# The last tile's middle row on ScalarE and accumulating transfers, and TensorE's first tile added by VectorE

## The chip, the cores and the metric

The kernel runs on one core of a Trainium2 chip. The metric is the device time of one execution in microseconds, taken as a median over runs. The engines are named as in the profile: PE (TensorE, with PEld for its weight loads), DVE (VectorE), ACT (ScalarE), POOL (GpSimd) and SP (SyncE, which here only issues transfers). [...]

## The reference, cut to what matters

The input is `x` of shape (16, 384, 32, 32) in fp32. Two layers follow each other:

```
x = x + attention(groupnorm32(x))     # qkv, 8 heads of 48, softmax over 1024 positions, projection, bias
x = x + depthwise7x7(groupnorm32(x))  # w_sym = mean of the weight's four rotations, padding 3
```

Group norm takes mean and variance over 12 channels times 1024 positions of one image. Because the symmetric weights are a mean over four rotations, a tap and its mirror image are equal under a half turn, and the kernel uses that to halve the multiplications.

## The kernel before, in words

An image has 1024 positions (N) and its 384 channels are three tiles of 128 partitions, so a tile `(b, k)` is 128 x 1024 in fp32, 512 KB. A hand-written planner issues the work: `catch_up` and `tap` hand out VectorE's queue, `after` puts a function at a due time, `conv_piece` hands out TensorE's part of the convolution, and loops of the kind "while something is not there, catch_up" hold back what is issued next. Each engine then runs its own queue strictly in this order, and waits on semaphores between engines.

Attention of image b overlaps with the convolution of image b-1. What concerns this document is the tail: when the last image's attention is done, its convolution has no more attention to hide behind. The three tiles of the last image, and one of the image before it, are handled in two ways.

- Three tiles, `PE_TILES` = (14, 2), (15, 2) and (15, 1), are convolved on TensorE. `conv_load` has SP issue eight transfers a half tile (`sh`), `conv_on_pe` runs 28 small matmuls for each half a = 0, 1 of a tile into PSUM (`ps_conv`), `conv_take` has ScalarE copy the half to SBUF (`rows`), and `conv_perm` brings its rows into order with four matmuls against a permutation (`ps_rows`). For (14, 2) and (15, 2) ScalarE then writes the result into `conv` and POOL issues a transfer that adds it into the tile `x1`, and SP stores the tile. For the last one, (15, 1), `conv_add` has VectorE add the result into `x1` in four pieces, and ACT issues the two halves of the store.
- The tile `LAST` = (15, 0) is convolved on VectorE by `fold_ops`. `sides` are three sums (later differences) of the padded tile shifted left and right by j = 1, 2, 3. For the middle row (dy = 0) of the kernel the centre product and three products of the sides are added into the output `out_t` (which is `x1s[LAST]`). For the rows dy = 1, 2, 3 the even part gathers in `rows_e` (first product by ScalarE in `fold_first`, three more by VectorE in `into`), and `shifted` adds it into `out_t` shifted up and shifted down. The odd part gathers in `rows_o` and is added one way and subtracted the other way.

The last image's group norm is folded in afterwards. The convolution runs on the raw `x1`, and at the end it is scaled by `sc[:, k, 0]`, while a border term carries the mean. Statistics: `st.moments` on ScalarE (two passes for each of three tiles), `st.average` on TensorE (seven one-column matmuls, twice), `spread_of` on VectorE between the two, then `scale_of` with a power on POOL, then `factors`, which adds the border to `ends["x"]` (the tile `rest`, a copy of the padded tile) by an accumulating transfer. `other_borders` does the same for (15, 2) and (15, 1). `whole` is VectorE's pass `out_t * scale + rest`. In the kernel before it stands in the middle of the last list of operations, and what is added after it (two row pairs) carries the scale or its negative (`minus`) as a factor.

`fast_end` writes the order of all this. Its part before the change that the prediction follows:

```
fold_first(n, 0)
st.moments(padded_view(n), 0)            # then the other two tiles, then the copy "rest"
while pe_conv[0][0] < b: conv_piece(False)     # the rest of (14, 2)
conv_piece(False)                              # (15, 2), first half
st.average(late["masks"], 0, mean)             # first statistics
conv_piece(False)                              # (15, 2), second half, taps 0 to 4
st.average(late["masks"], NK, st.d)            # second statistics
for p in first: conv_perm(*p)                  # rows of (14, 2)
```

Of the kernel before, what the change touches and what calls it, by code (L numbers as in the profile page):

```python
# [10 lines left out]
F32 = mybir.dt.float32  # L11
# [5 lines left out]
P = 128  # L17
# [28 lines left out]
def kernel(  # L46
# [96 lines left out]
    def run(general):  # L143
        tag = "g" if general else "f"
        with ExitStack() as stack:
# [706 lines left out]
            def fold_ops(b, k, i):  # L852
# [16 lines left out]
                scale = []  # L869

                def shifted(src, dy, op, half=None):
                    lo, hi = max(0, -dy) * W, (H - max(0, dy)) * W
                    if half is not None:
                        lo, hi = (lo, N // 2) if half == 0 else (N // 2, hi)
                    dst, src = out_t[:, lo:hi], src[:, lo + dy * W : hi + dy * W]
                    if scale:
                        w = scale[0] if op == ALU.add else scale[1]
                        vec.scalar_tensor_tensor(dst, src, w, dst, ALU.mult, ALU.add)
                    else:
                        vec.tensor_tensor(dst, dst, src, op)  # L880
# [17 lines left out]
                if (b, k) == LAST:  # L898
                    outs.append((ts, lambda: first(grid(out_t), padded_view(i), e(0, 0))))
                else:  # L900
                    outs.append((full, lambda: into(grid(out_t), padded_view(i), e(0, 0))))
# [25 lines left out]
                if (b, k) == LAST:  # L927
                    outs.pop()
                    for half in range(2):
                        outs.append(  # L930
                            (
                                0.7,
                                lambda half=half: (
                                    shifted(rows_o[0], -PAD, ALU.subtract, half),
                                    half_store(b, k, half),
                                ),
                            )
                        )
# [16 lines left out]
                if (b, k) == LAST:  # L955

                    def begin(n, dy, j):
                        nc.scalar.activation(rows_o[n], sides[slot[j]], AF.Identity, scale=o(dy, j))  # L958
# [5 lines left out]
                    def minus_begin():  # L964
# [3 lines left out]
                    ops = [op for op in ops if op[1] not in [f for _, f in (*sums[12:], *outs[10:])]]  # L968
# [3 lines left out]
                        (full, lambda: (sums[14][1](), other_borders()), None),  # L972
# [155 lines left out]
            def conv_perm(b, k, a):  # L1128

                nonlocal clock  # L1130
                if a == 0:
                    return
                pss[b, k] = psum(f"ps_rows_{b}_{k}")
                for half in range(2):
                    part = slice(64 * half, 64 * half + 64)
                    for row in range(2):
                        nc.tensor.matmul(
                            pss[b, k][part, row, :],
                            lhsT=perm[:, row],
                            rhs=shs[b, k][:, half, :],  # L1140
                            start=True,
                            stop=True,
                        )
# [5 lines left out]
                if b == B - 1:  # L1149
                    while "borders" not in late:  # L1150
                        catch_up(now() + 0.5)
                    nc.scalar.activation(
                        by_rows(t), grids(pss[b, k]), AF.Identity, scale=ends["st"].sc[:, k, 0:1]
                    )
                else:
                    nc.scalar.copy(by_rows(t), grids(pss[b, k]))
# [422 lines left out]
            def conv_piece(rows=True):  # L1579
# [14 lines left out]
                elif a and (b, k) == PE_TILES[-1]:  # L1594
                    conv_take(b, k, 0)
# [62 lines left out]
            def fast_end(b):  # L1658
# [11 lines left out]
                fold_first(n, 0)  # L1670
                st.moments(padded_view(n), 0)
# [9 lines left out]
                loads(1)  # L1681
                conv_piece(False)
# [7 lines left out]
                catch_up(clock)  # L1690
                st.average(late["masks"], NK, st.d)
# [164 lines left out]
```

## Time and profile before

| | us |
|---|---|
| median of 3 runs | 2836.43 (2835.36 to 2836.66) |
| the profiled execution's own time | 2835.83 |
| its span, first to last instruction | 2834.1 |
| what lies around the span | 1.7 |
| start of the last image's convolution on VectorE (first `side`) | 2781.46 |
| end of `conv_add`, the last work of an engine | 2826.01 |

In the profile a line of the timeline gives the start in us, the duration, the engine and source line, the operation, output and input, the count, and in brackets the time that the engine stood idle just before and what ended the idling. SPq, ACTq and POOL with DMA_DIRECT2D are issues of transfers. A count of 56 on PE is 28 matmul instructions, since an fp32 one is recorded twice. Successive instructions of one engine overlap by some 0.1 us, so costs are better read from start to start.

| stretch of the tail (us) | PE busy | DVE busy | ACT busy | DMA share |
|---|---|---|---|---|
| 2781.00 to 2804.20 | 23.20 | 23.06 | 14.56 | 0.51 |
| 2804.20 to 2811.00 | 6.80 | 6.73 | 3.67 | 0.51 |
| 2811.00 to 2829.90 | 13.31 | 13.85 | 7.53 | 0.90 |

### The profile page before, as it was taken

The numbers are of one execution on the slowest core, as the hardware profiler recorded it, in microseconds if no ns is written. First come the engines' busy times: TensorE is split into PE (matmuls) and PEld (weight loads), VectorE is DVE, ScalarE is ACT, GpSimd is POOL, SyncE is SP. The second block draws the span as 40 slices with busy tenths as digits, with TensorE's granted clock in tenths as the row PEclk, the third lists the DMA queues.
The fourth block names the chain that finished last, engine by engine and source line by source line (L and its number), as shares of the span: only waits on it lengthen the run. The fifth ranks groups of instructions, "written<-read, shape, count | busy, mean of one in ns | idle before, by whom it ended". The sixth has DMA issues, their size and how long they took to land. (4 is left out here: it accounts for less than half of the span.)

```text
span 2834.1 us, 46121 instructions
## 1 busy us (share of the span) xinstructions
PE 2822.4 (100%) x19344; PEld 1118.1 (39%) x19344; DVE 2080.6 (73%) x2266; ACT 1664.3 (59%) x1954; POOL 277.6 (10%) x450
## 2 busy tenths in 40 slices
PE   9999999999999999999999999999999999999998
PEld 5343343433434334343443434334343343434433
DVE  4503968959598595976959689595985959769788
ACT  3637647375574756647476473755747566474653
POOL 4201011310100001010010100101000010100111
PEclk9999999999999999999999999999999999999999
DMA  6522131211212112131120302112121121211224
GB/s 240 187 38 49 31 78 27 54 50 45 64 32 44 50 44 65 34 71 35 38 64 27 82 24 51 50 45 64 32 44 50 44 65 34 65 42 37 72 72 136
DMA packets 75562, 168.21 MB, mean 59 GB/s; under 512 B 32368, under 2 KB 34352, under 8 KB 73808
## 3 DMA queue, kind: packets, MB, share of 16 engines
q0 software_dynamic: 33856, 111.00, 15.1%
q1 hardware_dynamic: 40912, 53.11, 6.9%
q8 instruction: 154, 2.52, 0.4%
q10 hardware_dynamic: 576, 1.05, 0.1%
q14 instruction: 64, 0.52, 0.1%
HBM read 112.37 MB, written 27.43 MB: 49 GB/s over the span
## 5 line engine op out<-in xcount | busy, mean ns | idle before, releaser
L642 ACT ACTIVATE e<-ps_s 128x1024 f32<-128x1024 f32 x1024 | 1021.3, 1029 | 448.0 <-PE ps_s L634 447.4
L634 PE MATMUL ps_s<-qk 48*64 48x512 f32 x8192 | 1034.5, 589 | 0.0
L654 PE MATMUL acc<-e,v 64*64 64x512 f32 x8192 | 1034.0, 588 | 0.0
L861 DVE TENSOR_TENSOR side<-padded 128x1024 f32<-128x1024 f32 x270 | 329.8, 1222 | 339.7 <-ACT padded L832 339.7
L864 DVE SCALAR_TENSOR_TENSOR rows_e<-side,even,rows_e 128x1024 f32<-128x1024 f32 x405 | 510.5, 1276 | 85.6 <-ACT rows_e L843 84.0
L654 PEld LDWEIGHTS acc<-e,v 64*64 64x64 f32 x8192 | 308.9, 132 | 571.6 <-issue 571.4
L634 PEld LDWEIGHTS ps_s<-qk 48*64 48x64 f32 x8192 | 307.6, 132 | 574.7 <-issue 525.3
L563 PE MATMUL ps_qk<-x,wqk 128*128 128x512 f32 x1152 | 501.2, 593 | 0.0
L563 PEld LDWEIGHTS ps_qk<-x,wqk 128*128 128x128 f32 x1152 | 217.6, 190 | 276.7 <-issue 272.2
L880 DVE TENSOR_TENSOR x<-x,rows_e 128x992 f32<-128x992 f32 (+2 forms) x270 | 312.0, 1156 | 0.0
L880 DVE TENSOR_TENSOR x<-x,rows_o 128x992 f32<-128x992 f32 (+2 forms) x266 | 305.6, 1149 | 3.0
L570 ACT COPY qk<-ps_qk 128x1024 f32<-128x1024 f32 x96 | 97.2, 1012 | 318.6 <-PE ps_qk L563 318.5
L589 PE MATMUL ps_v<-wv,x 128*128 128x384 f32 x768 | 252.6, 486 | 0.0
L715 PE MATMUL ps_proj<-o,wp 128*128 128x512 f32 x540 | 234.2, 592 | 0.0
L609 ACT COPY v<-ps_v 64x384 f32<-64x384 f32 x256 | 121.4, 474 | 122.6 <-PE ps_v L589 120.0
L589 PEld LDWEIGHTS ps_v<-wv,x 128*128 128x128 f32 x768 | 145.9, 190 | 108.2 <-issue 14.3
L990 POOL DMA_DIRECT2D out<-x x44 | 24.8, 564 | 1543.0 <-DVE x L880 1542.5
L864 DVE SCALAR_TENSOR_TENSOR rows_o<-side,odd,rows_o 128x1024 f32<-128x1024 f32 x135 | 172.8, 1280 | 2.0 <-ACT rows_o L958 0.5
L864 DVE SCALAR_TENSOR_TENSOR x<-side,even,x 128x1024 f32<-128x1024 f32 x135 | 172.8, 1280 | 0.0
L715 PEld LDWEIGHTS ps_proj<-o,wp 128*128 128x128 f32 x540 | 102.6, 190 | 126.2 <-issue 118.4
L723 ACT ACTIVATE x<-ps_proj,bp 128x1024 f32<-128x1024 f32 x45 | 50.1, 1113 | 167.6 <-PE ps_proj L715 167.6
L843 ACT ACTIVATE rows_e<-padded,even 128x1024 f32<-128x1024 f32 x135 | 146.8, 1166 | 0.0
(178 smaller groups left out, 1049.2 us busy)
## 6 DMA issues: line engine op xcount, KB each, us to landing
x<-in_x POOLq DMA_DIRECT2D x90, 512.0 KB, 5.4
inv<-inv SPq DMA_DIRECT2D x126, 256.0 KB
out<-x POOLq DMA_DIRECT2D x44, 512.0 KB, 2.9
xs<-in_x POOLq DMA_DIRECT2D x42, 512.0 KB, 6.7
qk<-qk POOLq DMA_DIRECT2D x96, 128.0 KB, 4.1
o<-o SPq DMA_DIRECT2D x180, 32.0 KB
sh<-v SPq DMA_DIRECT2D x32, 128.0 KB
x<-in_x SPq DMA_DIRECT2D x6, 512.0 KB
```

What stands on the lines that cost most here:

```text
L563: nc.tensor.matmul(ps[:, h, :], lhsT=wqk[:, k, s, t, :], rhs=xns[b][:, k, h * HALF : (h + 1) * HALF], start=(k == 0), stop=(k == NK - 1),)
L570: nc.scalar.copy(halves(qks[u][:, s, :]), ps)
L589: nc.tensor.matmul(ps[:, j, 0:C], lhsT=xns[b][:, k, t * P : (t + 1) * P], rhs=wv[:, k, :], start=(k == 0), stop=(k == NK - 1),)
L609: nc.scalar.copy(dst[:, :, 0 : HEADS // 2 * (D + 1)].rearrange("p k (h d) -> p k h d", d=D + 1)[:, :, :, 0:D], src.rearrange("p k (h d) -> ...
L634: nc.tensor.matmul(ps[64 * c : 64 * c + 64, a, :], lhsT=qk[r, 1, 64 * kb : 64 * kb + 64], rhs=qk[r, 0, h * HALF : (h + 1) * HALF], start=True,
L642: nc.scalar.activation(es[n], ps, AF.Exp, scale=SCALE)
L654: nc.tensor.matmul(accs[a][64 * j : 64 * j + 64, :], lhsT=v[rows, kb, c : c + 64], rhs=e[rows, j, :], start=(kb == 0), stop=(kb == 2 * NT ...
L715: nc.tensor.matmul(ps[:, h, :], lhsT=wp[:, t, o * P : (o + 1) * P], rhs=os_[b, t // 2][:, t % 2, h * HALF : (h + 1) * HALF], start=(t == 0 ...
L843: nc.scalar.activation(grid(rows_e[dy - 1]), padded_view(i), AF.Identity, scale=even[:, k, dy, 0:1],)
L861: vec.tensor_tensor(grid(sides[n]), padded_view(i, j), padded_view(i, -j), op)
L864: vec.scalar_tensor_tensor(dst, src, w, dst, ALU.mult, ALU.add)
L880: vec.tensor_tensor(dst, dst, src, op)
```

## The change

All edits lie in the tail, behind the last softmax step; up to there both kernels issue the same instructions.

1. The middle row of `LAST`: the centre product is now one ScalarE activation into `x1s[LAST]`, and the three products of the sides are ScalarE activations into tiles of their own (`row_1`, `row_2`, `row_3`), all ahead of `st.moments`. Three accumulating transfers of POOL sum them: `row_1` into x1, `row_3` into `row_2`, and when both have landed `row_2` into x1. VectorE no longer takes part.
2. The order of VectorE's list for `LAST`: three sums, nine even row sums, then the three differences, then the shifted adds. The factor pass `whole` goes to the end, in two halves with a store each, so all shifted adds before it are plain adds and the negative factor goes.
3. Tile (14, 2): in place of four matmuls, a copy and an accumulating transfer, `conv_rows_by_dma` has SP issue 16 transfers of 32 KB from `rows` into a tile `planes`, and `rows_add` has VectorE add that into x1 behind the two halves of `whole`; SP's store of the tile comes after it.
4. `conv_perm`'s two loops over rows and halves are exchanged.
5. TensorE's pieces of the second half of a last-image tile: taps 0 to 2, 2 to 4, 4 to 7 in place of 0 to 4, 4 to 7. The first of them comes ahead of the first statistics, the second between first and second statistics, and the third after the second statistics, once the scale has been issued.
6. `other_borders` is issued after the adds of the second odd row instead of at its beginning.

The diff, cut to its core:

```diff
-                def shifted(src, dy, op, half=None):
+                def shifted(src, dy, op):
                     lo, hi = max(0, -dy) * W, (H - max(0, dy)) * W
...
-                def whole():
-
-                    scale.extend((ends["st"].sc[:, k, 0:1], ends["minus"]))
-                    vec.scalar_tensor_tensor(out_t, out_t, scale[0], ends["x"], ALU.mult, ALU.add)
+                    dst = out_t[:, lo:hi]
+                    vec.tensor_tensor(dst, dst, src[:, lo + dy * W : hi + dy * W], op)
+
+                def whole(h):
+
+                    half, s = slice(h * HALF, (h + 1) * HALF), ends["st"].sc[:, k, 0:1]
+                    vec.scalar_tensor_tensor(
+                        out_t[:, half], out_t[:, half], s, ends["x"][:, half], ALU.mult, ALU.add
+                    )
...
+                    def row_product(j):
+                        t = flat(epool.tile([P, 2, HALF], F32, tag="e", name=f"row_{j}"))
+                        nc.scalar.activation(t, sides[j - 1], AF.Identity, scale=e(0, j))
+                        ends["row", j] = t
+                        if j == 1:
+                            nc.gpsimd.dma_start(out_t, t, accum_op=ALU.add)
+                        if j == 3:
+                            nc.gpsimd.dma_start(ends["row", 2], t, accum_op=ALU.add)
+                            nc.gpsimd.dma_start(out_t, ends["row", 2], accum_op=ALU.add)
...
-                    ops = [op for op in ops if op[1] not in [f for _, f in (*sums[12:], *outs[10:])]]
+                    ops = [(*f, {0: "x", 3: "rows"}.get(n)) for n, f in enumerate(sums[:12])]
                     ops += [
                         (full, lambda: side_begin(2, 0, 1), None),
                         (full, lambda: side_begin(3, 1, 2), None),
-                        (full, lambda: (sums[14][1](), other_borders()), None),
+                        (*sums[14], None),
+                        *((*outs[n], None) for n in range(4, 8)),
                         (*sums[16], None),
                         (*sums[18], None),
                         (*outs[10], None),
                         (full, minus_begin, None),
-                        (full, whole, None),
-                        (*outs[12], None),
+                        (*outs[8], None),
+                        (*outs[9], None),
+                        (full, lambda: (outs[12][1](), other_borders()), None),
                         (*outs[13], None),
                         (*sums[20], None),
-                        *((*f, None) for f in outs[14:]),
+                        (*outs[14], None),
+                        (full, lambda: shifted(rows_o[0], -PAD, ALU.subtract), None),
+                        *((0.7, lambda h=h: (whole(h), half_store(b, k, h)), None) for h in range(2)),
+                        (full, rows_add, None),
                     ]
...
+            def rows_add():
+
+                b, k = PE_TILES[0]
+                dst = by_rows(x1s[b, k])
+                nc.vector.tensor_tensor(dst, dst, grids(ends["planes"]), ALU.add)
+                store(b, k, slice(0, N), nc.sync)
...
+                if (b, k) == PE_TILES[0]:
+                    conv_rows_by_dma(b, k)
+                    return
                 pss[b, k] = psum(f"ps_rows_{b}_{k}")
-                for half in range(2):
-                    part = slice(64 * half, 64 * half + 64)
-                    for row in range(2):
+                for row in range(2):
+                    for half in range(2):
+                        part = slice(64 * half, 64 * half + 64)
                         nc.tensor.matmul(
...
+            def conv_rows_by_dma(b, k):
+
+                rows = epool.tile([P, 2, HALF], F32, tag="e", name=f"planes_{b}_{k}")
+                for half in range(2):
+                    for i in range(NG // 2):
+                        for row in range(2):
+                            first = 2 * CG * i + CG * (1 - row)
+                            nc.sync.dma_start(
+                                rows[64 * half + i : 64 * half + 64 : NG // 2, row, :],
+                                shs[b, k][first : first + CG, half, :],
+                            )
+                ends["planes"] = rows
...
-                    pe_conv.extend(((b, k, 0, 0, KS), (b, k, 1, 0, 4), (b, k, 1, 4, KS)))
+                    pe_conv.extend(((b, k, 0, 0, KS), (b, k, 1, 0, 2), (b, k, 1, 2, 4), (b, k, 1, 4, KS)))
                 loads(2)
                 fold_first(n, 0)
+                nc.scalar.activation(
+                    grid(x1s[LAST]), padded_view(n), AF.Identity, scale=even[:, 0, 0, 0:1]
+                )
+                while "row" not in ends or active[0][2] < 3:
+                    catch_up(vclock + 0.5)
+                for f in ends["row"]:
+                    f()
                 st.moments(padded_view(n), 0)
...
                 loads(1)
+                first = [perms.popleft() for _ in range(2)]
+                conv_piece(False)
                 conv_piece(False)
                 catch_up(clock)
                 mean, var = st.first
                 st.average(late["masks"], 0, mean)
...
-                after(1.5, 0.6, lambda: st.spread_of(mean, var))
-                first = [perms.popleft() for _ in range(2)]
+                after(4.5, 0.6, lambda: st.spread_of(mean, var))
                 conv_piece(False)
                 catch_up(clock)
+                while not hasattr(st, "d"):
+                    catch_up(now() + 0.5)
                 st.average(late["masks"], NK, st.d)
...
-                minus = st.more[:, 2 * NK :]
-                nc.vector.tensor_scalar(minus, st.sc[:, 0, 0:1], -1.0, None, ALU.mult)
-                ends.update(minus=minus, st=st)
+                ends.update(st=st)
```

More of the change, by code (lines that the diff above doesn't have):

```diff
@@ L867, in first @@
                     vec.tensor_scalar(dst, src, w, None, ALU.mult)
-                scale = []
-                def shifted(src, dy, op, half=None):
+                def shifted(src, dy, op):
                     lo, hi = max(0, -dy) * W, (H - max(0, dy)) * W
[L873 to L880, printed above, removed]
-                def whole():
-                    scale.extend((ends["st"].sc[:, k, 0:1], ends["minus"]))
-                    vec.scalar_tensor_tensor(out_t, out_t, scale[0], ends["x"], ALU.mult, ALU.add)
+                    dst = out_t[:, lo:hi]
[5 more added lines that the diff above has]
+                    )
                 def e(dy, dx):
@@ L897, in fold_ops @@
                     sums.append((full, lambda j=j: side(j, j - 1, ALU.add)))
[L898 to L901, printed above, removed]
+                outs.append((full, lambda: into(grid(out_t), padded_view(i), e(0, 0))))
                 for j in (1, 2, 3):
@@ L926, in fold_ops @@
                     out_rows(lambda n=n: rows_o[n % 2], dy, ALU.subtract)
-                if (b, k) == LAST:
-                    outs.pop()
-                    for half in range(2):
[L930 to L938, printed above, removed]
                 behind = [0, 1, 2, 3, 6, 6, 9, 9, 12, 12, 17, 17, 19, 19, 21, 21, 21]
@@ L955, in fold_ops @@
                 if (b, k) == LAST:
+                    ends["row"] = [lambda j=j: row_product(j) for j in (1, 2, 3)]
+                    def row_product(j):
[7 more added lines that the diff above has]
+                            nc.gpsimd.dma_start(out_t, ends["row", 2], accum_op=ALU.add)
                     def begin(n, dy, j):
@@ L1132, in conv_perm @@
                     return
+                if (b, k) == PE_TILES[0]:
+                    conv_rows_by_dma(b, k)
+                    return
                 pss[b, k] = psum(f"ps_rows_{b}_{k}")
-                for half in range(2):
-                    part = slice(64 * half, 64 * half + 64)
-                    for row in range(2):
+                for row in range(2):
+                    for half in range(2):
+                        part = slice(64 * half, 64 * half + 64)
                         nc.tensor.matmul(
@@ L1147, in conv_perm, with conv_out @@
                     return
-                t = tpool.tile([P, N], F32, tag="t", name=f"conv_{b}_{k}")
[L1149 to L1156, printed above, removed]
+                while "borders" not in late:
+                    catch_up(now() + 0.5)
+                conv_out(b, k, pss[b, k])
+            def conv_rows_by_dma(b, k):
[9 more added lines that the diff above has]
+                ends["planes"] = rows
+            def conv_out(b, k, rows):
+                t = tpool.tile([P, N], F32, tag="t", name=f"conv_{b}_{k}")
+                nc.scalar.activation(
+                    by_rows(t), grids(rows), AF.Identity, scale=ends["st"].sc[:, k, 0:1]
+                )
                 nc.gpsimd.dma_start(x1s[b, k], t, accum_op=ALU.add)
@@ L1593, in conv_piece @@
                     perms.append((b, k, a))
-                elif a and (b, k) == PE_TILES[-1]:
+                elif a and not first and (b, k) == PE_TILES[-1]:
                     conv_take(b, k, 0)
@@ L1667, in fast_end @@
                     conv_begin(st, b, k)
-                    pe_conv.extend(((b, k, 0, 0, KS), (b, k, 1, 0, 4), (b, k, 1, 4, KS)))
+                    pe_conv.extend(((b, k, 0, 0, KS), (b, k, 1, 0, 2), (b, k, 1, 2, 4), (b, k, 1, 4, KS)))
                 loads(2)
                 fold_first(n, 0)
+                nc.scalar.activation(
+                    grid(x1s[LAST]), padded_view(n), AF.Identity, scale=even[:, 0, 0, 0:1]
+                )
+                while "row" not in ends or active[0][2] < 3:
+                    catch_up(vclock + 0.5)
+                for f in ends["row"]:
+                    f()
                 st.moments(padded_view(n), 0)
@@ L1686, in fast_end @@
                 clock += 1.6
-                after(1.5, 0.6, lambda: st.spread_of(mean, var))
-                first = [perms.popleft() for _ in range(2)]
+                after(4.5, 0.6, lambda: st.spread_of(mean, var))
                 conv_piece(False)
                 catch_up(clock)
+                while not hasattr(st, "d"):
+                    catch_up(now() + 0.5)
                 st.average(late["masks"], NK, st.d)
```

## The prediction

> **What bounds the kernel now.** The page first: the edits all lie behind the last softmax step, so its whole-run shares only say that TensorE is never idle for long.
>
> ```profile
> span 2834.1 us, 46121 instructions
> PE 2822.4 (100%) x19344; PEld 1118.1 (39%) x19344; DVE 2080.6 (73%) x2266; ACT 1664.3 (59%) x1954; POOL 277.6 (10%) x450
> ```
>
> The chain of waits is one piece long (DVE L1167), so I read the timeline of the tail engine by engine. TensorE (start, duration, work):
>
> ```profile
> 2780.71 16.41 PE L1111 MATMUL ps_conv<-sh,mat 128*32 128x464 f32 x158
> 2797.05 1.72 PE L389 MATMUL ps_st_x<-mo_x,wv 128*128 128x1 f32 x14
> 2798.71 3.48 PE L1111 MATMUL ps_conv<-sh,mat 128*32 128x512 f32 x32
> 2802.12 1.72 PE L389 MATMUL ps_st_x<-d_x,wv 128*128 128x1 f32 x14
> 2803.77 1.94 PE L1137 MATMUL ps_rows<-rows,perm 128*64 128x512 f32 x8
> 2805.65 2.63 PE L1111 MATMUL ps_conv<-sh,mat 128*32 128x496 f32 x24
> 2815.77 5.90 PE L1111 MATMUL ps_conv<-sh,wqk 128*32 128x512 f32 x56
> 2821.60 2.70 PE L1137 MATMUL ps_rows<-rows,perm 128*64 128x512 f32 x8
> ```
>
> From 2780.7 to 2824.3 each piece starts where the last ends: no hole. VectorE at the end, and the last issues of POOL and ScalarE's queue:
>
> ```profile
> 2822.53 1.31 DVE L878 SCALAR_TENSOR_TENSOR x<-rows_o,mo_x,x 128x416 f32<-128x416 f32 x2
> 2824.35 1.66 DVE L1167 SCALAR_TENSOR_TENSOR x<-ps_rows,sc_x,x 128x256 f32<-128x256 f32 x4 [0.50 <-PE ps_rows L1137]
> 2820.33 0.85 POOL L1157 DMA_DIRECT2D x<-conv  x1 [3.87 <-DVE x L878]
> 2823.22 4.15 ACTq L1171 DMA_DIRECT2D out<-x  x4
> ```
>
> The final add (conv_add) waits 0.50 us for TensorE. So TensorE's dense run sets the end, with VectorE only 0.5 behind; from the add's end (2826.0) stores and closing take 8.1 us to the span's end. Work taken from VectorE alone buys at most 0.5. ScalarE is the engine that I read as spare, and it is where the change puts work:
>
> ```profile
> 2782.63 3.25 ACT L843 ACTIVATE rows_e<-padded,even 128x1024 f32<-128x1024 f32 x3
> 2785.78 1.06 ACT L318 ACTIVATE sq_x<-padded 128x1024 f32<-128x1024 f32 x1
> 2793.73 1.05 ACT L1675 COPY rest<-padded 128x1024 f32<-128x1024 f32 x1
> 2794.69 1.06 ACT L1126 COPY rows<-ps_conv 128x512 f32<-128x512 f32 x2
> 2797.21 0.58 ACT L1126 COPY rows<-ps_conv 128x512 f32<-128x512 f32 x1 [1.47 <-PE ps_conv L1111]
> 2810.27 2.18 ACT L958 ACTIVATE rows_o<-side,odd 128x1024 f32<-128x1024 f32 x2
> ```
>
> Before 2797.2 it is packed; its only slack there is the 1.47 us ahead of the copy of tile (15,2)'s first half.
>
> **VectorE.** Costs start to start. Removed: the L867 product (0.67), three L864 into x (3 x 1.20), the minus factor (0.1); two 960-wide L878 become plain adds (1.22 to 1.07 each: 0.3), the 928-wide ones also (2.5 to 2.1: 0.4). Added: rows_add, priced as L861's add of the same size, 1.13. The factor pass of 1.28 becomes two halves: 0. Sum: -4.0 us.
>
> **TensorE.** One block of four rows matmuls goes (2803.77 to 2805.65): -1.9. The loop in conv_perm is turned: for the last tile, three of four matmuls (it was two) now follow the copy of the second half; 1.94/4 gives +0.5. The convolution piece of (15,2), second half, is cut in two (0 to 2, 2 to 4), and the first cut moves ahead of the first statistics. In the changed kernel's instruction order that first cut waits for ScalarE's copy of the same tile's first half (one PSUM tile holds both halves). Before, that wait was covered by the statistics block; now nothing stands in front of it.
>
> **When ScalarE gets there.** Ahead of the moments it now has the first product (as L843: 3.15/3 = 1.05) and three row products (as L958: 2.18/2 = 1.09 each): +4.3. What followed moves with it: the moments start at 2790.1 instead of 2785.78, `rest` at 2798.05, (14,2)'s two copies at 2799.0, and (15,2)'s first half at about 2800.0 to 2800.55. TensorE finishes that half at 2797.05 and stands until 2800.6: **+3.5 us**. From there 8 matmuls (1.7), statistics (1.7), 8 more (1.7), second statistics at 2805.7 (2802.12 before), and the rest packed as before without the one block: last rows matmuls at 2823.3 (2821.60 before). Sum for TensorE: +3.5 - 1.9 + 0.5 = +2.1; conv_add starts at 2826.5, ends at 2828.1.
>
> VectorE's 4.0 us are lost on the way: it has its nine row sums and three differences done at 2799.3, then waits for the accumulating transfers and for the statistics that TensorE delivers at 2804.2, and again for L406 at 2807.5. It reaches conv_add at about 2823.3, three microseconds early, with rows_add inside that slack.
>
> **The transfers.** POOL issues three accumulating transfers in place of one (0.87 each). The third needs both others landed, so POOL stands for 5 us with nothing behind it until the factor's power at 2807.6: 0. The row is the landing of such a 512 KB transfer here: 5.4 us (L1157), 5.6 to 7.6 (L1722, two at once). The third product is written at 2790.2; at 5.4 twice the middle row is complete at 2801.0, at 7.6 twice at 2805.4. The trace of before has none beside the 32 `sh` loads (DMA share 0.51 from 2781 to 2804), so I take 5.4 to 6.6: 2801 to 2803.4. [...] It matters only past 2804.0: VectorE's add behind it (1.1) and the spread (0.5) must be done when TensorE asks at 2805.7. So 0 in the sum, and +1.4 at the far end.
>
> SP issues 16 small transfers behind the loads, from 2804.2. The rows lie between 0.34 (L1171) and 0.59 us (L1090) an issue: done by 2810 to 2814, wanted at 2822: 0; past 2822 each microsecond late eats the 3 us of slack first. If transfers in flight hold them up, +2 is the bound.
>
> Stores: ScalarE's border for (15,2) now stands behind its second copy and a product that needs VectorE's 2813.3; it ends at 2815.9 (POOL issued it at 2814.17), so the two accumulations and (15,2)'s store behind it move by +1.8, within the +2.1. (14,2)'s store, at 2811.7 before, goes behind that one: 0.5 MB more after 2827. Moved at the 347 GB/s of the last stretch it is 1.4 us; half-hidden beside the closing I take +0.4, bounds -1 (one of the four ACTq issues was long, 1322 ns, and may be short next time) and +1.4.
>
> **Sum.** +2.1 + 0.4 = +2.5 on the profiled execution's 2835.83: 2838.3. The median shown (2836.43) is 0.6 above that execution: **2838.9**.
>
> [...] Granted clock by stretch (stretch and its length, busy time of PE, PEld, DVE, ACT and POOL, granted clock, DMA share, GB/s):
>
> ```profile
> 8.46:11.88 3.42, 3.02 (x26) 2.62 (x24) 1.29 (x7) 0.00 (x0) 1.57 (x6) 1.00 1.04 397
> 11.88:15.29 3.41, 3.41 (x9) 2.74 (x9) 2.26 (x8) 1.24 (x1) 2.65 (x4) 0.50 0.41 97
> 2797.05:2803.77 6.72, 6.72 (x64) 4.21 (x60) 6.65 (x9) 0.58 (x1) 0.00 (x0) 1.00 0.52 173
> 2827.87:2834.10 6.23, 0.00 (x0) 0.00 (x0) 0.00 (x0) 0.00 (x0) 0.00 (x0) 0.50 0.22 78
> ```
>
> Today the tail keeps 1.00 and falls to 0.50 only 3.5 us after the last matmul. [...] But row two shows a halved window after one with 3.02 us of mostly one-column matmuls, so low work can suffice, and the hole with 1.7 us of statistics behind it is such a stretch. One halved window costs up to 1.7 us: 2840.6. I leave it out of the number and in the range.
>
> **Rivals.**
> - *Clock halves in the hole*, as just priced: about 2840.6. For: rows two and four. Against: the second statistics block of today did not trip it.
> - *Middle row lands late (slower).* Place: the first shifted add into x, ahead of the spread in VectorE's queue. It decides from a landing at 2804.0. Beside loads that already hold half of the DMA time, the three transfers could take 7.6 each with the second queued behind the first by 2 us: 2807.5, so TensorE waits 3.5 more, and in a second hole the clock is likelier to fall. +2.5 + 3.5 = 2842.4, with the clock 2844.1. Against: the loads use only 0.51 of the time and their data are wanted late.
> - *The copy does not hold TensorE* (ScalarE shorter than I price it): -1.9 + 0.5 + 0.4 = -1.0, 2835.4. The full -4.0 of VectorE, if nothing else were late, would be 2832.4, still within 0.2%, so a gain past 0.2% has no working here.
>
> **Numbers.** 0.2% is 5.7 us, about what a measurement of this kernel can tell from no change: faster is below 2830.8, slower above 2842.1. Forecast 0.43; clock 0.21 (a quarter of it with the DMA bounds past 2842.1); late landing 0.25 (nearly all slower); no hold 0.11 (up to 0.04 faster, for what I can't see). Together faster 0.04, same 0.66, slower 0.30. Range 2834.5 to 2845.0: below lies most of the no-hold case's far end, above the landings past 2807 with the clock down.
>
> **What would show it.** In the changed profile: a hole of about 3.5 us on TensorE before the first cut of (15,2), ended by ScalarE's rows copy; second statistics near 2805.7; conv_add waiting some 3 us, not 0.5, for TensorE; the middle row's landing between 2801 and 2803.4; clock 1.00 throughout. Wrong if TensorE has no hole there, if VectorE and not TensorE ends last, or if the first shifted add starts after 2804.

## The result, and the profile after

The changed kernel takes 2842.87 us (median of 8 runs, 2841.74 to 2846.84), the kernel before on the same chip 2835.89 (8 runs, 2835.06 to 2836.76). The measured ratio, which is not simply that of the two medians (1.0025), is 1.0028, with a 95% interval of 1.0019 to 1.0038. So it is slower by 7.0 us, clear of no change, and the lower end of the interval lies just under the 0.2% that the prediction took as the bound of its classes. The profiled execution took 2841.74 (before 2835.83), with a span of 2840.0 (before 2834.1), so the profile has 5.9 of the 7.0 us to explain.

TensorE in the timeline of the changed kernel's tail (start, duration, work, and in brackets the idle time ahead):

```profile
2780.72 16.41 PE L1115 MATMUL ps_conv<-sh,mat 128*32 128x464 f32 x158
2800.46 3.29 PE L1115 MATMUL ps_conv<-sh,mat 128*32 128x512 f32 x16 [3.33 <-DMA sh<-v]
2803.68 1.93 PE L389 MATMUL ps_st_x<-mo_x,wv 128*128 128x1 f32 x14
2805.54 1.84 PE L1115 MATMUL ps_conv<-sh,mat 128*32 128x480 f32 x16
2807.53 1.72 PE L389 MATMUL ps_st_x<-d_x,wv 128*128 128x1 f32 x14
2809.18 2.62 PE L1115 MATMUL ps_conv<-sh,mat 128*32 128x496 f32 x24
2825.13 2.71 PE L1144 MATMUL ps_rows<-rows,perm 128*64 128x512 f32 x8
```

There is a hole where the dense run was unbroken before, and behind it 16 matmul records that take 3.29 us where the next 16 take 1.84. Stretch by stretch (PE, PEld, DVE, ACT and POOL busy, granted clock, DMA share, GB/s), with the edges put where the granted clock changes:

```profile
2797.30:2800.71 3.41, 0.25 (x4) 0.16 (x8) 2.81 (x3) 3.41 (x8) 0.85 (x1) 1.00 0.68 208
2800.71:2804.13 3.42, 3.42 (x19) 0.89 (x11) 0.00 (x0) 1.78 (x2) 0.00 (x0) 0.50 1.03 195
2804.13:2807.54 3.41, 3.26 (x30) 1.82 (x30) 1.65 (x5) 0.00 (x0) 0.00 (x0) 1.00 0.76 206
```

The clock is halved for one stretch of 3.41 us. In the same stretch VectorE does nothing at all (0.00 us busy), and the DMA engines are busy throughout (share 1.03). The other queues, from the timelines of ScalarE, VectorE, POOL and SP:

```profile
2798.86 1.55 ACT L1130 COPY rows<-ps_conv 128x512 f32<-128x512 f32 x3
2805.82 1.19 DVE L872 TENSOR_TENSOR x<-x,rows_e 128x992 f32<-128x992 f32 x1 [5.71 <-DMA x<-row]
2827.92 1.23 DVE L986 TENSOR_TENSOR x<-x,planes 128x1024 f32<-128x1024 f32 x1 [2.51 <-DMA planes<-rows]
2829.06 1.65 DVE L1187 SCALAR_TENSOR_TENSOR x<-ps_rows,sc_x,x 128x256 f32<-128x256 f32 x4
2799.32 0.85 POOL L947 DMA_DIRECT2D x<-row  x1 [8.11 <-DMA row<-row]
2818.68 0.86 POOL L1750 DMA_DIRECT2D x<-border  x1 [3.58 <-ACT border L1749]
2824.30 0.85 POOL L1177 DMA_DIRECT2D x<-conv  x1 [3.37 <-DVE x L872]
2781.08 29.39 SPq L1094 DMA_DIRECT2D sh<-v  x32
2810.57 12.27 SPq L1166 DMA_DIRECT2D planes<-rows  x16
2830.91 1.93 SPq L1191 DMA_DIRECT2D out<-x  x2
```

The same queues before, SP's loads and POOL's issue of the border of (15, 2):

```profile
2781.07 23.07 SPq L1090 DMA_DIRECT2D sh<-v  x32
2814.17 0.85 POOL L1722 DMA_DIRECT2D x<-border  x1 [2.64 <-ACT border L1721]
```

Three chains come in late, one behind the other by a microsecond or so:

- **TensorE.** Hole, halved clock: its last rows matmuls end at 2827.84, 3.5 us later than before (2824.30).
- **Planes.** SP's loads last until 2810.5 (before 2804.1), the 16 plane transfers stand behind them, the last lands at 2827.84 by the trace's semaphore events. `rows_add` waits 2.51 us for it and holds `conv_add` 1.2 us longer than TensorE does. `conv_add` ends at 2830.71 (before 2826.01: +4.7).
- **Border and stores.** POOL issues the border of (15, 2) at 2818.68 (before 2814.17). The second accumulation into the same tile, L1177, waits for that border to land. The profile names VectorE there, but the instruction's waits are for the border's landing and for ScalarE's product; the border's landing, at 2823.79, is the later. L1177 lands at 2830.86, SP's store of (15, 2) goes at 2830.91 and (14, 2)'s behind it; the last store lands at 2836.3 (before 2830.9: +5.4).

`conv_add` is 4.7 us later, the time from there to the last landing 0.7 longer, and the closing after that landing 0.5 longer: 5.9. Why the closing grew stays open.

### The profile page after: what moved, and what is told of

Read it like the earlier page. It is cut to its first block, busy times and chain, and to the rows that moved or that the text cites. A ratio compares the mean times of both kernels' runs of the same rounds, so it can differ in the third digit from the quotient of the medians.

```text
span 2840.0 us, 46131 instructions
## 1 busy us (share of the span) xinstructions
PE 2822.5 (99%) x19336; PEld 1118.1 (39%) x19336; DVE 2077.6 (73%) x2262; ACT 1668.1 (59%) x1957; POOL 273.6 (10%) x452
## 4 chain that ended last, share of the span: by engine, by line
PE 98%; SPq 1%; DMA 0%; DVE 0%; issue 0%; ACT 0%; DVEq 0%
PE ps_s L634 31%; PE acc L654 31%; PE ps_qk L563 18%; PE ps_v L589 9%; PE ps_proj L715 8%; SPq L1094 1%; PE ps_proj_last L763 1%; SPq L1166 0%; PE warm L1533 0%; DMA planes<-rows 0%; PE ps_st_x L423 0%; PE ps_sum L742 0%; DVE x L1187 0%; DVE x L986 0%; PE ps_conv L1115 0%
## 5 line engine op out<-in xcount | busy, mean ns | idle before, releaser
L723 ACT ACTIVATE x<-ps_proj,bp 128x1024 f32<-128x1024 f32 x45 | 50.1, 1114 | 167.5 <-PE ps_proj L715 167.5
```

## The experiments

Every kernel was timed beside the kernel before, with 6 to 11 runs each. Times are medians; the ratio and its interval are to the kernel before on the same chip. That one took 2835.9 and 2835.6 us beside the first two groups of four, and 2839.2 beside e9 to e11 and 2839.1 beside e12, which ran on two other chips. So kernels of different groups are compared by ratio, and the times that the expectations of e9 to e12 name are some 3 us low for those chips. The last three columns are of the profiled execution, counted from the start of TensorE's dense run (2780.71 before), in us: TensorE's last rows end, `conv_add` ends, the last store lands.

| kernel | us | ratio | PE | conv_add | landing |
|---|---|---|---|---|---|
| before | 2835.89 | 1 | 43.6 | 45.3 | 50.2 |
| changed | 2842.87 | 1.0028 (1.0019, 1.0038) | 47.1 | 50.0 | 55.6 |
| e1 rows back on TensorE | 2843.46 | 1.0031 (1.0019, 1.0043) | 50.7 | 52.4 | 57.5 |
| e2 middle row on VectorE | 2839.98 | 1.0015 (1.0006, 1.0024) | 46.0 | 47.7 | 53.6 |
| e3 cuts as before | 2843.10 | 1.0025 (1.0015, 1.0035) | 44.8 | 52.6 | 57.2 |
| e4 no middle-row transfers | 2841.34 | 1.0022 (1.0013, 1.0031) | 53.4 | 55.1 | 59.9 |
| e5 PSUM tile of its own | 2844.73 | 1.0030 (1.0018, 1.0042) | 52.1 | 53.8 | 59.2 |
| e6 filler matmuls | 2843.01 | 1.0028 (1.0017, 1.0038) | 48.5 | 50.2 | 56.5 |
| e7 = e2 + e3 | 2841.11 | 1.0019 (1.0010, 1.0028) | 44.9 | 46.7 | 54.2 |
| e8 = e7, add on POOL | 2842.71 | 1.0024 (1.0015, 1.0033) | 43.2 | 48.3 | 54.6 |
| e9 tail reordered | 2845.77 | 1.0025 (1.0016, 1.0035) | 53.4 | 55.1 | 59.5 |
| e10 = e7 + spread + tail | 2838.47 | 1.0001 (0.9992, 1.0010) | 41.7 | 45.7 | 51.0 |
| e11 = e10, rows on TensorE | 2838.44 | 0.9999 (0.9990, 1.0008) | 43.6 | 45.3 | 50.1 |
| e12 = e7 + spread | 2842.28 | 1.0014 (1.0005, 1.0023) | 41.7 | 45.8 | 53.5 |

One caution for the three columns: the profiled executions of e4, e5 and e9 are ones in which the clock stayed halved for 17.07 us (below), so their columns are larger than most of their own runs would show.

**Theories.** H: the hole behind ScalarE's copy, with the halved clock. T: the accumulating transfers of the middle row hold up the loads, and with them the planes. S, later E: the end, where borders, accumulations and stores stand in a row.

### One part undone at a time: e1 to e4

e1, (14, 2)'s rows back on TensorE (no planes, no `rows_add`; the copy to `conv` and its accumulating transfer come back too and are not printed here):

```diff
-                if (b, k) == PE_TILES[0]:
-                    conv_rows_by_dma(b, k)
-                    return
...
-                        (full, rows_add, None),
```

> The rows of tile (14,2) go back to four permutation matmuls, ScalarE's copy and an accumulating transfer; no planes, no rows_add. Theory H (TensorE's hole behind ScalarE's copy, with the halved clock) leaves the hole: TensorE gets its 1.9 us block back, which now fills time in which it would wait for the spread, so the last rows matmuls stay near 2825 to 2827 and the time near 2841 to 2843. Theory S (the planes and the store order at the end are what costs) says that conv_add no longer stands behind rows_add's 2.5 us wait and (14,2)'s store goes out early: 2838 to 2840.

Measured 1.0031, no better than the change. `conv_add` no longer waits for planes, but 5.97 us for TensorE, which has its 1.9 us of work back and stood at half clock twice in this execution, for 3.41 us each from 2799.30 and from 2809.54. S alone is out; the median (2843.46) is 0.5 above H's 2841 to 2843.

e2, the middle row back on VectorE (first product and three adds; ScalarE's products and POOL's three transfers go):

```diff
+                    outs[0] = (ts, lambda: first(grid(out_t), padded_view(i), e(0, 0)))
+                    for n in range(4):
+                        ops.insert(2 * n + 1, (*outs[n], None))
...
-                for f in ends["row"]:
-                    f()
```

> The middle row goes back to VectorE (its first product and three adds); no products on ScalarE, no accumulating transfers. Theory H: ScalarE's copy comes some 4 us earlier, the hole of 3.33 us and the halved clock go: TensorE ends its last rows near 2821 to 2822. Theory T (the accumulating transfers hold up the loads behind them and the middle row) says that the loads on SP end near 2804 instead of 2810.5 and the planes are there in time. Both: 2835 to 2838; under S alone (end of kernel) it would stay above 2840.

Measured 1.0015: 2.9 us less than the changed kernel, the largest part that any of these four gives back, but not all (the intervals still overlap). The loads end at 2802.4 and the planes land by 2814.8, as T says. TensorE's first hole shrinks to 0.72 us. But it now stands 1.61 us for the spread (VectorE's L402), which the change puts behind the differences, and the clock is halved after that too, from 2805.94 to 2809.35. The time is 2 us above the 2835 to 2838 expected.

e3, the second half of (15, 2) cut as before, with the statistics in front:

```diff
-(b, k, 1, 0, 2), (b, k, 1, 2, 4), (b, k, 1, 4, KS)
+(b, k, 1, 0, 4), (b, k, 1, 4, KS)
...
-                conv_piece(False)
```

> The second half of (15,2) is again cut into taps 0 to 4 and 4 to 7, with the first statistics ahead of it. Theory H: the statistics fill 1.7 us of the hole, it shrinks to 1.6 us or less and the clock stays 1.00. If H set the end, the time falls by 3 to 4 us to about 2839; if T sets it (middle row landed at 2805.8, spread near 2807.5, planes at 2827.8), TensorE only waits at the second statistics instead and the time stays within 1 us of 2842.9.

H's part comes half true: TensorE waits only 0.64 us within the statistics and 0.91 ahead of the cut and ends 2.3 us sooner (44.8 for 47.1), but the clock is halved all the same, for one stretch from 2799.65. The time doesn't move: 2843.10. VectorE's timeline of this kernel says why:

```profile
2830.37 1.23 DVE L986 TENSOR_TENSOR x<-x,planes 128x1024 f32<-128x1024 f32 x1 [5.53 <-DMA out<-x]
```

The wait ended with the landing of the last planes transfer at 2830.29 by the trace (the name in brackets is of a store on the same semaphore). With TensorE out of the way the planes set the end. They even landed 2.6 us later after the start than in the changed kernel (49.8 for 47.1). The traces say what came with it: with TensorE sooner, POOL's first border transfer goes out at 2811.72 instead of 2814.20, beside more of the plane transfers. The three plane transfers issued before it landed 2.0 us after their issue, the last one 6.7 us after.

e4 leaves the three accumulating transfers out, so the side products of the middle row are missing from the last tile; ScalarE still makes them:

```diff
-                        if j == 1:
-                            nc.gpsimd.dma_start(out_t, t, accum_op=ALU.add)
-                        if j == 3:
-                            nc.gpsimd.dma_start(ends["row", 2], t, accum_op=ALU.add)
-                            nc.gpsimd.dma_start(out_t, ends["row", 2], accum_op=ALU.add)
```

> Leaves out the three accumulating transfers, so that the three side products of the middle row are missing from the last tile; ScalarE's products stay. Theory T: the loads on SP end near 2804, VectorE's first shifted add no longer waits 5.7 us, the planes land before 2822: 2 to 4 us less, about 2839 to 2841. Theory H: the hole of 3.3 us behind ScalarE's copy and the halved clock stay, so TensorE's last rows matmuls stay near 2825 and the time near 2842.

Measured 1.0022, 1.5 us less, well within the intervals. T's mechanism is there: the loads end at 2803.1, the planes are complete by 2815.7, VectorE doesn't wait for the middle row. And H's is there untouched, in TensorE's timeline and in the stretches of the profiled execution:

```profile
2800.95 2.87 PE L1110 MATMUL ps_conv<-sh,mat 128*32 128x512 f32 x16 [3.32 <-ACT rows L1125]
```

```profile
2801.62:2805.03 3.41, 3.41 (x18) 1.50 (x11) 0.07 (x1) 1.36 (x2) 0.00 (x0) 0.50 0.52 171
```

With none of the middle row's transfers about, the hole is 3.32 us, and the releaser is ScalarE's copy. So ScalarE's added work alone makes the hole, as predicted. In this execution the clock then stayed halved for five stretches, 17.07 us, and it took 2847.12, where eight of the other ten runs took 2840.29 to 2842.97.

### The hole and the clock by themselves: e5 and e6

e5 gives the second half of (15, 2) its own PSUM tile, so its first cut doesn't wait for the copy:

```diff
-                        ps = psum(f"ps_conv_{b}_{k}")
-                        pss[b, k, 0], pss[b, k, 1] = ps[:, 0, :], ps[:, 1, :]
+                        ps = psum(f"ps_conv_{b}_{k}_{a}")
+                        if (b, k) == PE_TILES[1]:
+                            pss[b, k, a] = ps[:, a, :]
```

> The second half of (15,2) is summed in a PSUM tile of its own, so that its first cut no longer waits for ScalarE's copy of the first half. If that copy ends the hole (theory H, as predicted), TensorE starts when the load has landed, about 2799.5 instead of 2800.4, the hole falls from 3.3 to about 2.4 us and the time by up to 0.9, to about 2842. If the load ends the hole (the profile names it), nothing moves: 2842.9.

```profile
2798.60 3.07 PE L1118 MATMUL ps_conv<-sh,mat 128*32 128x512 f32 x16 [2.02 <-DMA sh<-v]
```

The copy did end the hole: without it the cut starts 1.3 us sooner after the start of the dense run (18.4 for 19.7). But now the load ends it, at 2.02 us: the transfers had pushed that load's landing from 2794.0 (kernel before) to 2799.5 (changed kernel). The hole has two causes side by side, and H had named one. No time is won (1.0030): the clock fell all the same, for 17.07 us in the profiled execution.

e6 puts ten filler matmuls into the hole:

```diff
+                warm_2 = psum("warm_2")
+                for n in range(10):
+                    nc.tensor.matmul(
+                        warm_2[:, n % 2, 0:C], lhsT=ident, rhs=wp[:, 0, :], start=True, stop=True
+                    )
```

> Ten filler matmuls of 128x384 into an unused PSUM tile stand on TensorE ahead of the first cut of (15,2)'s second half; nothing reads them. Clock theory: the granted clock stays 1.00 through the tail, the first cut takes 1.8 instead of 3.3 us. The second statistics still wait for the spread, which waits for the middle row (2805.8), and the planes still land near 2827.8, so the profiled run falls by at most 1, but the scatter between 2841.7 and 2846.8 shrinks, if the long ones are longer stretches of halved clock: median about 2841.5. If the clock isn't what scatters, runs near 2846 stay.

The clock stays 1.00 through the tail, and the first cut takes 1.85 us. The filler was too long: it lasted 6.72 us, so the cut began 3.3 us later after the start of the dense run than in the changed kernel. TensorE ends 1.4 us later than in the changed kernel, and the time is the same (1.0028). About 2841.5 was expected: a miss for the median. For the scatter it says something: of the changed kernel's eight runs three lie at 2846.3 to 2846.8, all three with a mean clock of 0.995, the other five at 0.997 to 0.998; with the filler all eight have 0.998 or 0.999 and only one lies above 2845. That one, 2847.06 at 0.998, has another cause that stays open.

### Hole and transfers both undone: e7 and e8

e7 takes the edits of e2 and e3 together.

> Cuts as before (0 to 4, 4 to 7, statistics in front) and the middle row on VectorE; what is left of the change is the plain adds with the factor in the last pass, and (14,2)'s rows by transfers with rows_add. H and T together say that hole, halved clock and late planes are all gone: TensorE's last rows start near 2820, planes land near 2814, VectorE sets the end (conv_add 2824.3 to 2826.0): 2836 to 2837, level with before. If the rows by transfers cost something by themselves (theory S: store order at the end), 2837.5 to 2839.

Measured 1.0019, where 2836 to 2837 was expected: H and T are not all of it. TensorE and the stretch ahead of the halved clock:

```profile
2803.03 1.72 PE L389 MATMUL ps_st_x<-d_x,wv 128*128 128x1 f32 x14 [1.41 <-DVE d_x L402]
```

```profile
2802.43:2805.84 3.41, 2.81 (x26) 2.06 (x30) 3.34 (x8) 1.27 (x2) 0.47 (x1) 1.00 0.37 112
```

TensorE waits 1.41 us for the spread, which `after(4.5, ...)` puts behind two of the differences, and one stretch of half clock follows, from 2805.84 to 2809.25. Yet `conv_add` ends only 1.4 us later than before. The last store lands 4.0 later: POOL's border is issued at 2816.45, the second accumulation into (15, 2) lands at 2829.42, and SP's two stores go from 2829.47.

e8 is e7 with `rows_add` on POOL ahead of the borders:

```diff
-                nc.vector.tensor_tensor(dst, dst, grids(ends["planes"]), ALU.add)
+                nc.gpsimd.tensor_tensor(dst, dst, grids(ends["planes"]), ALU.add)
```

> As the one with both cuts and middle row as before, but rows_add runs on POOL, between the border of the last tile and the two other borders, and (14,2)'s store follows it. VectorE loses 1.1 us and the store goes out near 2818: conv_add near 2823.2, 2834 to 2835.5, about 1 below the kernel before. If POOL's add is long or slows VectorE beside it, 2836 or more.

Slower than the kernel before instead (1.0024), where 2834 to 2835.5 was expected; from e7 it can't be told apart. POOL's queue, then VectorE's:

```profile
2816.56 2.37 POOL L988 TENSOR_TENSOR x<-x,planes 128x1024 f32<-128x1024 f32 x1 [5.19 <-DMA planes<-rows]
```

```profile
2816.63 4.50 DVE L872 TENSOR_TENSOR x<-x,rows_o 128x960 f32<-128x960 f32 x2
```

POOL waits 5.19 us for the planes, with both borders behind it, and VectorE's two adds beside POOL's take 4.50 us instead of 2.35.

### The end by itself: e9 to e12

e9 is the changed kernel with the borders issued ahead of the third `rows_o` product and (14, 2)'s store on ScalarE's queue:

```diff
-                        (*outs[10], None),
+                        (full, lambda: (outs[10][1](), other_borders()), None),
                         (full, minus_begin, None),
...
-                        (full, lambda: (outs[12][1](), other_borders()), None),
+                        (*outs[12], None),
...
-                store(b, k, slice(0, N), nc.sync)
+                store(b, k, slice(0, N), nc.scalar)
```

> The changed kernel with only its tail reordered: the two other borders are made on ScalarE ahead of its third rows_o product (as before) and not behind it, and (14,2)'s store stands on ScalarE's queue instead of behind (15,2)'s on SP. Theory E (the chain border of (15,2) issued 2818.7, landed 2823.8, second accumulation into the same tile issued 2824.3, landed 2830.9, then (15,2)'s store and behind it (14,2)'s, last landing 2836.3): the border is issued near 2815.5, the second accumulation lands near 2827, the last landing is near 2834, and the time is 1.5 to 2.5 less, 2840.5 to 2841.5. If conv_add, held by the planes, sets the end alone, 2842.9 stays.

Measured 1.0025, as the changed kernel. The order of the end alone doesn't bring the time back. Its profiled execution had 17.07 us of half clock, so it can't say how much the end gained; as a test of E by itself it is inconclusive. e10, e11 and e12 test E where the other chains are gone. e10 is e7 with this tail and the spread early again:

```diff
-                after(4.5, 0.6, lambda: st.spread_of(mean, var))
+                after(1.5, 0.6, lambda: st.spread_of(mean, var))
```

> Cuts as before, middle row on VectorE, the spread placed after 1.5 instead of 4.5, and the reordered tail; left of the change are the plain adds with the factor in the last pass and (14,2)'s rows by transfers with rows_add. If the late spread (TensorE waited 1.4 for it in the run with cuts and middle row as before) and the tail's chain are what was left, TensorE has no hole, conv_add runs 2824.5 to 2826.0, the stores land by 2831: 2834.5 to 2836.5, level with the kernel before. If rows by transfers cost something else, 2838 or more.

> As the one with everything reordered, but (14,2)'s rows go back to TensorE's matmuls and the accumulating transfer; left of the change are the plain adds with the factor in the last pass alone. TensorE is the bound again, dense to 2824.3, and VectorE has 0.7 us more room: 2835.3 to 2836, level with the kernel before. If it is above 2838, the new order of VectorE's passes is itself the cost.

> Cuts as before, middle row on VectorE, spread after 1.5 instead of 4.5; the tail keeps the change's order (borders behind the third rows_o product, (14,2)'s store behind (15,2)'s on SP). It splits the gap between the run with cuts and middle row as before (0.19% over the kernel before) and the one with the tail reordered too (level). If TensorE's 1.4 us hole for the spread and the halved clock behind it made the gap, 2835.5 to 2837, level with the kernel before. If the tail's chain of border, second accumulation and two stores on SP made it, TensorE has no hole and the clock stays 1.00, but the second accumulation still lands near 2829 and the last store near 2834: 2839 to 2841.

e10 is level with the kernel before (1.0001), and so is e11 (0.9999), in which (14, 2)'s rows are back on TensorE as well. So neither the new order of VectorE's passes nor the rows by transfers costs anything once the rest is undone. e12 has everything of e10 but the tail, and is at 1.0014. In the profiled executions of e10 and e12 TensorE and VectorE do the same: no hole, last rows 41.7 us after the start, `conv_add` 45.7 and 45.8. The difference is all in the queues of POOL and SP, e12 first, then e10:

```profile
2818.49 0.88 POOL L1745 DMA_DIRECT2D x<-border  x1 [7.13 <-ACT border L1744]
2823.65 0.87 POOL L1180 DMA_DIRECT2D x<-conv  x1 [2.88 <-DMA x<-border]
2830.63 1.70 SPq L1194 DMA_DIRECT2D out<-x  x2
```

```profile
2812.03 0.87 POOL L1746 DMA_DIRECT2D x<-border  x1 [0.50 <-ACT border L1745]
2819.49 0.87 POOL L1181 DMA_DIRECT2D x<-conv  x1 [5.18 <-DVE x L872]
2825.83 0.34 SPq L1195 DMA_DIRECT2D out<-x  x1
```

With the borders behind ScalarE's third `rows_o` product, which waits 5.47 us for VectorE's adds, POOL issues (15, 2)'s border 6.5 us later, the second accumulation lands 4.8 later (2830.58 for 2825.77), and the last store 2.5 later after the start (53.5 for 51.0). The spans differ by 3.2 (2839.5 for 2836.3), since the closing behind the last landing is longer too (3.9 for 2.9). So the tail is enough to make the kernel slower by 0.14% with TensorE dense, and the chain is shown at work. The tail holds two edits, the border's place and (14, 2)'s store on ScalarE's queue, and no run splits them. The intervals of e10 and e12 touch (1.0010 and 1.0005), so its size rests on the profiles more than on the times.

No version beats the kernel before: e10 takes 1.9 us off TensorE and none off the end: VectorE then arrives at `conv_add` last, without a wait (`conv_add` ends at 45.7, before 45.3).

**What follows.** The changed kernel lost on three chains of about the same length, so that undoing one shows another: TensorE's hole made smaller (e3), the planes end it; the middle row undone (e2, e7), the late spread and the stores; these undone too (e12), the stores alone; all undone (e10), level. Only the stores stand alone in a run; what TensorE's chain or the planes would cost by themselves is read from the profiles and was not timed.

## Why the prediction was right or wrong

It said 2838.9, no change as the likeliest class, with slower at 0.30. The time lies 4.0 above it and 0.8 past the bound of slower (2842.1). It is inside the stated range (2834.5 to 2845.0) only because the range left room for the rivals; the sum itself missed. By its own signs it was wrong too: the first shifted add started at 2805.82, past 2804; the clock did not stay at 1.00; and `conv_add` waited not for TensorE but for VectorE's own `rows_add`, which the planes held. The profiled execution, predicted at 2838.3, took 2841.74: the prediction was 3.4 short, and these are split below.

- **Bound.** Right that TensorE's dense run and `conv_add` set the end before. What it left out is that (15, 2)'s chain of border, accumulation and store ended level with it: before, the second accumulation landed at 2825.74 and SP's store went at 2825.80, `conv_add` ended at 2826.01. It moved that chain by 1.8, inside TensorE's delay, and took the planes as a want at 2822 with 3 us to spare; so, apart from +0.4 for the stores, neither stood in the sum.
- **ScalarE and the hole.** As priced: moments at 2789.96 (said 2790.1), `rest` 2797.92 (2798.05), copy done 2800.41 (2800.55), hole 3.41 us from start to start (+3.5). Its cause was half the truth: the load that the cut needs as well landed at 2799.54, 0.9 us ahead of the copy, and e5 shows it taking over.
- **Rows block and turned loop.** The block's -1.9 came as said. The turned loop's +0.5 didn't: the last block takes 2.71 us for 2.70.
- **Clock.** This is the term left out of the number; no run shows a hole of 3.3 us or more that leaves the clock at 1.00. It came: +1.7 at the first cut and the statistics behind it (3.22 and 1.86 us from start to start, for 1.71 and 1.65). With +0.3 of waiting for the spread TensorE stood at 3.41 + 1.7 + 0.3 - 1.9 = +3.5, not +2.1. The trace had shown a halved window after one with 3.02 us of low work (one- and two-column statistics for the most part, not one-column alone as the prediction says); that row should have weighed more, and the 0.21 given to it was too low, as far as these runs go: e1 to e5, e7 and e9 all show it in their profiled executions.
- **Middle row.** Said 2801 to 2803.4, far end 2805.4; measured 2805.8. The three transfers took 6.8, 8.4 and 6.5 us from issue to landing, where 5.4 to 6.6 was taken from rows without loads beside them. The rival's place was right (5.71 us at the first shifted add) and its price wrong: TensorE, late by its own clock, had to wait 0.3, not 3.5.
- **The loads**, which the step missed. It asked what the loads do to the transfers, not what the transfers do to the loads: SP's 32 loads end 6.3 us later. e2 and e4 (no accumulation) end them at 2802.4 and 2803.1.
- **Planes.** Said 0.34 to 0.59 us an issue, done by 2810 to 2814; measured 0.77 an issue from 2810.6, last landing 2827.84. Priced 0 with a bound of +2; cost 1.2. That SP's queue starts late was the loads' doing. The last transfer landed 5.6 us after its issue, beside the accumulations of the borders; the first seven, issued ahead of the borders or with the first of them, landed after 2.0. In e2 and e5, where the borders come behind or with the last plane transfer, that one too landed after 2.0.
- **Stores.** Border issue said to move by 1.8, within TensorE's 2.1; it moved by 4.5, as the product ahead of it needs VectorE's adds, which end at 2815.75 where the prediction had 2813.3. Priced +0.4; cost 1.2.

Sum: clock, spread and loop (3.5 for 2.1) give 1.4, planes 1.2, stores 0.8: the 3.4. What came was the first rival and the second together, priced at 2844.1, but the second reached the end by the loads and the planes and not by TensorE's wait, as it was priced. VectorE's 4.0 us were lost as said, though later than said: it was ready for `conv_add` at 2826.5 by its own work (2825.4 plus `rows_add`), not at 2823.3.

## What to carry to other kernels

When a tail ends on one engine, list every chain that ends within a few microseconds of it, down to the landing of the last store, with its slack, before moving work; here there were three. With the stores alone left (e12) the kernel was still slower than before, and with all three undone (e10) it was level and not faster. When work goes from an engine to accumulating transfers, ask what stands behind them in every queue and in the DMA engines: here the loads (29.4 us of issues, 21.7 in e2) and the small transfers (the last landed 5.6 us after its issue, the first seven after 2.0) paid most, not the add that asked for the sum. And an experiment that undoes one of several equal chains can show nothing in the time (e3); read where the chain ends in its profile, and then undo them together.

## What the hardware showed that was not expected

- **Clock.** In these traces the stretches of half clock in the tail last whole multiples of 3.41 us (3.41 in the changed kernel, 17.07 in e4), and so do those of full clock that were read between them (6.83 in e1, 27.31 in the changed kernel): a grid that does not start with the hole (in the changed kernel the hole begins at 2797.1, the halved stretch at 2800.71). A stretch with 2.81 us of TensorE busy, 1.7 of it one-column statistics, stood ahead of a halved one (e7), as did one with 0.25 (changed kernel). In e4 TensorE was busy for all 3.41 us of a halved stretch, 1.28 of it statistics, and the clock stayed down for four more. In the changed kernel the clock was back at 1.00 behind the halved stretch, which has 2.97 us of convolution. Where the hole falls on the grid seems to decide whether and for how long the clock falls; that is the author's reading, which these runs do not settle. In e7 and e8 TensorE runs the same instructions up to its 1.4 us wait, which begins 21.5 us after the start. In e7 an edge of the grid (2802.43) falls into the wait, and the stretch up to the next edge, with 2.81 us busy, is followed by one halved stretch. In e8 the 3.41 us up to 2804.24 hold the wait whole, with 2.01 us busy, and the clock stays at 1.00 in them and in the 3.41 us behind. One stretch cost TensorE 1.7 us (changed kernel), five cost it 6.3 more (from the first cut to the last rows 33.7 us in e4, 27.4 in the changed kernel). The changed kernel's runs at 2846 fit the longer case by their mean clock (0.995, as in e4's profiled execution); none of them was profiled.
- **POOL beside VectorE.** One POOL add of 2.37 us went with 2.15 us more for VectorE's two adds beside it, 4.50 (e8) where the same two took 2.35 (changed kernel, e10). Why they are slower side by side was not measured.
- **Accumulating transfers beside loads.** The three transfers of the middle row, 512 KB each, took 6.5 to 8.4 us to land in the changed kernel; in the three stretches shown above the DMA share is 0.68 to 1.03 at only 195 to 208 GB/s. The loads beside them were held up: SP's 32 issues took 29.4 us for 21.7 in e2. The 32 KB plane transfers paid as well: 1.9 to 2.1 us from issue to landing ahead of the borders' accumulations, up to 5.9 beside them.
